# Folding two halves of a PSUM sum with a copy and an add, and turning it with transposes, in a graph attention network

## The chip, the cores and the metric

The kernel runs on one core of one Trainium2 chip. The metric is the device time of one launch in microseconds, as the median of several timed runs; less is better. Beside the timed runs there is one profiled run, from which all views of the profile come.

## The reference

Four layers of a graph network follow one another on 3327 nodes with 256 features each. The adjacency matrix has 3327 x 3327 entries, about 0.5% of them ones. Layer 0 is a simple attention that fills in the features; layers 1 to 3 are transformer layers, masked by the adjacency:

```python
qkv = layer_norm(x, g1, be1) @ w_qkv            # q, k, v: 8 heads of 32
scores = einsum('nhd,mhd->hnm', q, k) * SCALE
scores = where(adj != 0, scores, -inf)
attn = softmax(scores, axis=-1)
out = einsum('hnm,mhd->nhd', attn, v).reshape(n, 256)
x = x + out @ w_proj + b_proj
h2 = layer_norm(x, g2, be2)
x = x + gelu(h2 @ w1 + b1) @ w2 + b2            # 256 -> 1024 -> 256
```

Only the neighbours of a node count for its row of `out`. The change touches one place: between `out` and `out @ w_proj`.

## The kernel before

The kernel first reads the adjacency, does layer 0, and makes for each node a list of its neighbours. The nodes are sorted by their number of neighbours and cut into 26 blocks of 128. A block `b` has `CAPS[b]` neighbour slots (40 for the first, 24 to 10 for the others); a slot is one neighbour of each of the 128 nodes. A group is four slots. For each slot an indirect DMA, issued by GpSimd, gathers 128 rows of keys and values from DRAM into a ring of ten group buffers:

```python
def issue(self):
    ...
    t = ring.tile([P, GS * KVW[1]], FP, tag="kv", ...)        # ten buffers
    for s in range(n):                                        # up to 4 slots
        nc.gpsimd.indirect_dma_start(out=t[:, s, :], in_=kv[L], ...)   # L1226
```

VectorE multiplies keys by queries and reduces them to scores; ScalarE takes the exponentials; VectorE multiplies the values by the weights. TensorE then adds the slots up, two at a time: a product of the identity with 512 columns (two slots of 256) is accumulated in a PSUM bank `po`. At the end the bank's left half holds the sum of the even slots, its right half that of the odd ones. The rows of a block are nodes, the columns features:

```python
def values(self, b, s0):
    ...
    if s0 == 0:
        while len(self.po) > 1:            # two banks: a third block waits for the first
            self.short.pop(0)()
        self.po[b] = ps_o.tile([P, 512], FP, tag="o", ...)
    vw = work.tile([P, GS * D], FP, tag="vw", bufs=3, ...)
    nc.vector.tensor_mul(vw, v, wp)                                    # L1289
    for s in range(0, n, 2):
        m = min(2, n - s) * D
        nc.tensor.matmul(self.po[b][:, :m], ident, vw[:, s * D:s * D + m], ...)   # L1294
    self.issue()
    if s0 + GS >= S:
        self.short += self.block(b)
```

When the last group of a block is summed, its short steps are put in a queue: copy the bank to SBUF, bring it into the transposed form that the projection wants as its stationary operand, copy that, project, add to `x`.

```python
def block(self, b):
    ...
    def copy():
        c["o"] = work.tile([P, 2 * D], FP, tag="o", ...)
        nc.scalar.copy(c["o"], self.po[b])                             # L1312

    def turn():
        pt = self.po[b]
        for k in range(2):
            for h in range(2):
                k0 = h * D + k * P
                nc.tensor.matmul(pt[:, k * P:(k + 1) * P], c["o"][:, k0:k0 + P], ident,
                                 start=(h == 0), stop=(h == 1))        # L1319

    def copy_T():
        c["oT"] = work.tile([P, 2 * P], FP, tag="oT", ...)
        nc.scalar.copy(c["oT"], self.po[b][:, :2 * P])                 # L1324

    def project():
        ps = self.po[b][:, D:]
        nc.tensor.matmul(ps, ones_bf[:96, :], bias3[:, 0, :], start=True, stop=False)   # L1328
        for k in range(2):
            nc.tensor.matmul(ps, c["oT"][:, k * P:(k + 1) * P], w["w_proj"][:, k, :],
                             start=False, stop=(k == 1))               # L1330

    def add():
        nc.vector.tensor_add(x, x, self.po.pop(b)[:, D:])              # L1334
        n2.stats(chunk.index(b), x)
        if b == chunk[-1]:
            self.long += self.chunk(chunk, n2)     # the feed-forward part of up to 4 blocks
            ...
    return [copy, turn, copy_T, project, lambda: None, add]
```

The product of `turn` with the identity as the moving operand transposes a 128 x 128 piece; two of them, one from each half, accumulate into one place, so the halves are added while they are turned.

The feed-forward part of a chunk of blocks (norm, `up` into banks `pu` at L1373, `gelu` on ScalarE at L1379, `down` into `py` at L1396, transposes back into `pd` at L1410, the next layer's queries, keys and values at L1426) makes up the long queue. The loop takes a turn per group: scores, values of an earlier group, then steps of both queues. The order of instructions on each engine is as the program writes it.

```python
def some(self):
    if self.short:
        self.short.pop(0)()
    self.credit = min(self.credit + self.rate, 8.0)
    while self.long and self.credit > 0:
        cost, step = self.long.pop(0)
        self.credit -= cost
        step()
    if self.short:
        self.short.pop(0)()

def run(self):
    ...
    for k, b in enumerate(ORDER):          # blocks with few and many slots in turn
        for g in slots[b]:
            self.scores(*g)                                            # L1248, L1249
            if g == slots[b][-1]:
                self.softmax(b)
                ...
            for _ in range(2 if len(todo) > NBUF // 2 or b == 0 else 1):
                if todo and wait[todo[0][0]] > 1:
                    value()
            self.some()
        ...
```

Of the kernel before, what the change touches and what calls it, by code (L numbers as in the profile page):

```python
# [8 lines left out]
FP = mybir.dt.float32  # L9
# [8 lines left out]
P = 128  # L18
N = 3327
D = 256  # L20
# [503 lines left out]
def sparse_path(ctx, tc, ins, out, dram, flag):  # L524
    nc = tc.nc
# [3 lines left out]
    ident = const.tile([P, P], FP, name="s_ident")  # L529
# [93 lines left out]
    with tc.tile_pool(name="a", bufs=1) as a, tc.tile_pool(name="aw", bufs=2) as aw, \  # L623
# [44 lines left out]
        o = 0  # L668
# [364 lines left out]
        for i in range(NB):  # L1033
# [8 lines left out]
            k = 1 if i < NB - 2 else 2  # L1042
# [54 lines left out]
        for i in range(NB):  # L1097
            nc.tensor.matmul(pp[:, :2 * NB], oh_lo[:, i, :],
                             ids[:, i, :, :].rearrange("p a b -> p (a b)"),
                             start=(i == 0), stop=(i == NB - 1))  # L1100
# [35 lines left out]
    work = ctx.enter_context(tc.tile_pool(name="b_work", bufs=2))  # L1136
# [63 lines left out]
    class Layer:  # L1200
# [101 lines left out]
        def block(self, b):  # L1302
            L, w, c = self.L, self.w, {}
            x = t2[:, b, :D]
            chunk = CHUNK[b]
            if b == chunk[0]:
                self.n2 = Norm(len(chunk), f"f{L}_{b}")
            n2 = self.n2

            def copy():  # L1310
                c["o"] = work.tile([P, 2 * D], FP, tag="o", name=f"o_{L}_{b}")
                nc.scalar.copy(c["o"], self.po[b])  # L1312

            def turn():
                pt = self.po[b]
                for k in range(2):
                    for h in range(2):
                        k0 = h * D + k * P
                        nc.tensor.matmul(pt[:, k * P:(k + 1) * P], c["o"][:, k0:k0 + P], ident,  # L1319
                                         start=(h == 0), stop=(h == 1))  # L1320

            def copy_T():
                c["oT"] = work.tile([P, 2 * P], FP, tag="oT", name=f"oT_{L}_{b}")
# [13 lines that stand above are left out]
                    self.long += self.chunk(chunk, n2)  # L1337
                    at = ORDER.index(b) + 1
                    turns = sum(len(slots[i]) for i in ORDER[at:at + CB])
                    turns = 5 if at == NB - 1 else turns - 2  # L1340
                    self.rate = sum(cost for cost, _ in self.long) / max(turns, 1)

            return [copy, turn, copy_T, project, lambda: None, add]

        def chunk(self, blocks, n2):
            L, w, nxt = self.L, self.w, self.nxt
# [221 lines left out]
```

## Time and profile before

| what | value |
|---|---|
| timed, median of 3 | 2904.16 us (2901.46 to 2905.93) |
| profiled execution, span | 3329.9 us |
| mean granted TensorE clock in it | 0.791 |
| stage before the attention layers, in the profile | about 660 us |
| the three attention layers, in the profile | about 2670 us |

The profiled execution is longer than the timed ones. PE is TensorE's matmul row and PEld its weight loads, DVE is VectorE, ACT is ScalarE, POOL is GpSimd. A row of a group names the line, the engine, the operation, what is written from what, and the count, then busy time and mean duration, then the time the engine stood idle just before and what ended it. A row of a wait names who waited for whom, the sum in us, how often, and the longest. "issue" is time in which an engine waited for nothing that the profile shows; "remote" and "another core or an unknown queue" are releasers that the profile can't name.

### The profile page before, as it was taken

What the parts mean: (1) busy time and instruction counts of PE and PEld (TensorE: products, weight loads), DVE (VectorE), ACT (ScalarE), POOL (GpSimd) and SP (SyncE); (2) the same over time, 40 slices, a digit from 0 to 9 for tenths busy, and PEclk for the clock granted to TensorE, in tenths of its full rate; (3) what the DMA queues carried; (4) which work ended last, traced back from release to release, by engine and by line L of the source; (5) the groups of instructions that cost most, each with busy time, mean ns of one, the idle gap of its engine ahead of it and who ended that gap; (6) DMA issues with size and microseconds to landing.
All of it is one profiled execution on the core that took longest, in us unless ns stands there. A gap on an engine that the chain in (4) does not pass through costs nothing.

```text
span 3329.9 us, 22700 instructions
## 1 busy us (share of the span) xinstructions
PE 2138.1 (64%) x6859; PEld 1150.0 (35%) x6859; DVE 1957.7 (59%) x4063; ACT 767.3 (23%) x1335; POOL 1362.9 (41%) x1461
## 2 busy tenths in 40 slices
PE   4566666135678677774356887878733656767566
PEld 4444444013334333342123333333421323323234
DVE  3977774545666746743546667676444656557453
ACT  3344442001222222221012222222310211212111
POOL 3000000364555645511645555456035465556550
PEclk9676667567788889787678898888876887888788
DMA  4233321464556646533645556556145454545450
GB/s 175 103 109 109 121 76 53 139 185 139 156 154 178 186 133 168 167 71 95 176 130 151 150 156 173 148 153 179 31 134 159 133 169 137 161 137 165 140 142 13
DMA packets 144482, 453.73 MB, mean 136 GB/s; under 512 B 29521, under 2 KB 40156, under 8 KB 141021
## 3 DMA queue, kind: packets, MB, share of 16 engines
q0 software_dynamic: 113056, 370.26, 39.7%
q1 hardware_dynamic: 9834, 53.90, 4.6%
q10 hardware_dynamic: 21458, 28.02, 2.3%
q8 instruction: 56, 0.92, 0.1%
q14 instruction: 78, 0.64, 0.1%
HBM read 420.64 MB, written 31.42 MB: 136 GB/s over the span
## 4 chain that ended last, share of the span: by engine, by line
PE 20%; DVE 14%; issue 13%; POOL 9%; another core or an unknown queue 9%; DMA 3%; ACT 2%; DVEq 0%; POOLq 0%; SPq 0%; ACTq 0%
POOL kv L1226 9%; PE po L1294 7%; DVE kv L1248 4%; PE pu L1373 4%; PE py L1396 3%; DVE vw L1289 3%; DVE sc L1249 3%; DMA kv<-kv,t 3%; PE pk L1426 2%; PE po L1330 1%; PE po L1319 1%; PE pq L1426 1%; DVE st_f L575 0%; DVE t L1334 0%
## 5 line engine op out<-in xcount | busy, mean ns | idle before, releaser
L1226 POOL DMA_INDIRECT kv<-kv,t x1344 | 1276.8, 950 | 1243.9 <-issue 532.1
L1294 PE MATMUL po<-vw,s_ident 128*128 128x512 f32 (+1 forms) x1380 | 790.8, 711 | 493.1 <-DVE vw L1289 350.3
L1294 PEld LDWEIGHTS po<-vw,s_ident 128*128 128x128 f32 x1380 | 298.4, 228 | 854.1 <-issue 497.5
L1248 DVE TENSOR_TENSOR kv<-kv,q 128x1024 f32<-128x1024 f32 (+3 forms) x363 | 413.0, 1138 | 137.5 <-DMA kv<-kv,t 50.4
L1334 DVE TENSOR_TENSOR t<-t,po 128x256 f32<-128x256 f32 x78 | 32.8, 420 | 677.3 <-PE po L1330 287.2
L1249 DVE TENSOR_REDUCE sc<-kv 128x32 f32<-128x1024 f32 (+3 forms) x363 | 414.1, 1141 | 13.5 <-DVE kv L1248 1.1
L1289 DVE TENSOR_TENSOR vw<-kv,w 128x1024 f32<-128x1024 f32 x333 | 371.8, 1128 | 76.7 <-remote 59.8
L1373 PE MATMUL pu<-fT,s_w 128*128 128x512 f32 (+3 forms) x768 | 318.2, 548 | 43.3 <-issue 21.3
L1396 PE MATMUL py<-gT,s_w 128*128 128x512 f32 (+2 forms) x672 | 285.6, 553 | 1.3 <-ACT gT L1379 1.3
L1373 PEld LDWEIGHTS pu<-fT,s_w 128*128 128x128 f32 x768 | 152.9, 210 | 194.7 <-issue 151.9
L1379 ACT ACTIVATE gT<-pu,pvb 128x512 f32<-128x512 f32 (+3 forms) x192 | 115.9, 609 | 310.4 <-PE pu L1373 168.7
L702 POOL MEMSET s_abf<- 128x1 bf16 x26 | 2.6, 104 | 434.8 <-PE s_ptb L714 251.3
L1312 ACT COPY o<-po 128x512 f32<-128x512 f32 x78 | 45.7, 586 | 547.9 <-PE po L1294 276.1
L1396 PEld LDWEIGHTS py<-gT,s_w 128*128 128x128 f32 x672 | 128.5, 194 | 125.4 <-issue 106.3
L1319 PE MATMUL po<-s_ident,o 128*128 128x128 f32 x624 | 101.7, 314 | 94.8 <-ACT o L1312 65.0
L714 PE MATMUL s_ptb<-s_ident_bf,s_abf 128*128 128x128 bf16 x676 | 76.5, 291 | 116.0 <-ACT s_aT L715 80.4
L1319 PEld LDWEIGHTS po<-s_ident,o 128*128 128x128 f32 x624 | 92.3, 221 | 137.4 <-ACT o L1312 88.1
L1330 PEld LDWEIGHTS po<-s_w_proj,oT 128*128 128x128 f32 x312 | 62.3, 222 | 184.3 <-issue 176.5
L1426 PE MATMUL pk<-s_w_qkv,nT 128*128 128x512 f32 x208 | 116.7, 690 | 10.6 <-issue 7.0
L1328 PE MATMUL po<-bias,s_ones_bf 96*128 96x256 bf16 x78 | 23.3, 299 | 155.2 <-issue 98.8
L724 DVE MAX8 cand<-s_v 128x8 f32<-128x208 bf16 x416 | 117.6, 361 | 0.9
L1324 ACT COPY oT<-po 128x256 f32<-128x256 f32 x78 | 29.1, 373 | 371.1 <-remote 215.1
(284 smaller groups left out, 2486.2 us busy)
## 6 DMA issues: line engine op xcount, KB each, us to landing
s_a<-in_adj_dram SPq DMA_DIRECT2D x25, 1663.5 KB
kv<-kv,t POOLq DMA_INDIRECT x1344
kv<-kvr ACTq DMA_DIRECT2D x52, 256.0 KB
kv<-s_kvr ACTq DMA_DIRECT2D x26, 256.0 KB
s_w<-in_L_gnn_w_dram SPq DMA_DIRECT2D x6, 1024.0 KB
t<-ql ACTq DMA_DIRECT2D x6, 592.0 KB
t<-s_x ACTq DMA_DIRECT2D x6, 512.0 KB
s_w_qkv<-in_L_gnn_w_qkv_dram SPq DMA_DIRECT2D x3, 768.0 KB
```

What stands on the lines that cost most here:

```text
L724: nc.vector.max(out=self.cand[:, s, :], in_=v[:, s, :])
L1226: nc.gpsimd.indirect_dma_start(out=t[:, s, :], out_offset=None, in_=kv[L], in_offset=bass.IndirectOffsetOnAxis(ap=t2[:, b, k:k + 1].bitcas ...
L1248: nc.vector.tensor_mul(k, k, self.q[b][:, None, :].to_broadcast([P, n, D]))
L1249: nc.vector.tensor_reduce(self.sc[b][:, s0:s0 + n, :], k.rearrange("p s (h d) -> p s h d", d=HD), AX.X, ALU.add)
L1289: nc.vector.tensor_mul(vw[:, :n * D].rearrange("p (s h d) -> p s h d", h=HEADS, d=HD), v, self.wp[b][:, s0:s0 + n, :, None].to_broadcast([ ...
L1294: nc.tensor.matmul(self.po[b][:, :m], ident, vw[:, s * D:s * D + m], start=(s0 + s == 0), stop=(s0 + s + 2 >= S), skip_group_check=True)
L1319: nc.tensor.matmul(pt[:, k * P:(k + 1) * P], c["o"][:, k0:k0 + P], ident, start=(h == 0), stop=(h == 1))
L1330: nc.tensor.matmul(ps, c["oT"][:, k * P:(k + 1) * P], w["w_proj"][:, k, :], start=False, stop=(k == 1))
L1373: nc.tensor.matmul(c["pu", f][:, :n], w["w1"][:, e, f * P:(f + 1) * P], c["hT"][:, e, :n], start=(e == 0), stop=(e == 1))
L1379: nc.scalar.activation(g[:, :n], c.pop(("pu", f))[:, :n], AF.Gelu_apprx_tanh, bias=w["b1"][:, f:f + 1])
L1396: nc.tensor.matmul(c["py"][e][:, :n], w["w2"][:, f, e * P:(e + 1) * P], g[:, :n], start=(f == 0), stop=last)
L1426: nc.tensor.matmul(ps[:, :c1 - c0], c["hT"][:, e, j * P:(j + 1) * P], nxt["w_qkv"][:, e, c0:c1], start=(e == 0), stop=(e == 1))
```

## The change

The halves are added before they are turned. ScalarE copies only the left half of the bank to SBUF, VectorE adds the right half to it in place, and TensorE turns the sum with two transposes in place of four accumulating products. `o` takes half the room in SBUF. It is for less work on TensorE and ScalarE, at the price of one more instruction on VectorE. The queue of short steps gets two empty places ahead of and behind the copy, so that the steps stand further apart.

```diff
             def copy():
-                c["o"] = work.tile([P, 2 * D], FP, tag="o", name=f"o_{L}_{b}")
-                nc.scalar.copy(c["o"], self.po[b])
+                c["o"] = work.tile([P, D], FP, tag="o", name=f"o_{L}_{b}")
+                nc.scalar.copy(c["o"], self.po[b][:, :D])
+
+            def fold():
+                nc.vector.tensor_add(c["o"], c["o"], self.po[b][:, D:])
 
             def turn():
-                pt = self.po[b]
                 for k in range(2):
-                    for h in range(2):
-                        k0 = h * D + k * P
-                        nc.tensor.matmul(pt[:, k * P:(k + 1) * P], c["o"][:, k0:k0 + P], ident,
-                                         start=(h == 0), stop=(h == 1))
+                    nc.tensor.transpose(self.po[b][:, k * P:(k + 1) * P],
+                                        c["o"][:, k * P:(k + 1) * P], ident)
 ...
-            return [copy, turn, copy_T, project, lambda: None, add]
+            return [lambda: None, copy, lambda: None, fold, turn, copy_T, project, lambda: None, add]
```

## The prediction

> **What bounds the kernel now.** I read four views, in this order: busy time by engine, the waits, the chain that ended last (whole, then inside the layers), and the groups of the lines that change. One number comes first. The profiled execution takes 3329.9 us and the timed one 2904.16 us, so some 426 us of what the profile shows is not in the time to be predicted.
>
> Busy time by engine over the whole span:
>
> ```profile
> PE 2138.1 (64%) x6859; PEld 1150.0 (35%) x6859; DVE 1957.7 (59%) x4063; ACT 767.3 (23%) x1335; POOL 1362.9 (41%) x1461
> ```
>
> No engine is full. The first 660 us belong to the stage that reads the adjacency, which the change doesn't touch; the three attention layers share the other 2670 us. By stretch (columns: stretch, length, then busy us and instructions of PE, PEld, DVE, ACT, POOL, then the granted clock, DMA share and GB/s), the middles of the three layers and one layer's start and end look like this:
>
> ```profile
> 900.00:1400.00 500.00, 382.96 (x989) 180.46 (x988) 314.14 (x554) 127.02 (x281) 273.18 (x289) 0.85 0.59 165
> 1560.00:1700.00 140.00, 43.58 (x98) 20.30 (x98) 78.37 (x114) 9.27 (x22) 85.32 (x89) 0.62 0.57 164
> 1700.00:2280.00 580.00, 445.24 (x1177) 217.08 (x1178) 369.39 (x618) 138.44 (x242) 307.12 (x324) 0.87 0.54 156
> 2280.00:2440.00 160.00, 122.85 (x374) 68.99 (x372) 71.65 (x148) 40.55 (x75) 33.17 (x35) 0.85 0.30 73
> 2700.00:3200.00 500.00, 337.90 (x870) 161.52 (x870) 311.09 (x475) 95.16 (x158) 288.20 (x304) 0.83 0.53 154
> ```
>
> In the middles TensorE is busiest (77%, 77%, 68%), VectorE follows with 62 to 64%. GpSimd looks lower (53 to 58%), but each gather has 950 ns busy and an "issue" gap of about 300 ns after it, so a gather takes 1.25 us of GpSimd: the 304 GpSimd instructions of the last of these stretches, nearly all gathers, are 380 of 500 us, 76%. TensorE and GpSimd are about equally near to being a bound. The chain says the same. Over the whole span, by engine:
>
> ```profile
> PE 20%; DVE 14%; issue 13%; POOL 9%; another core or an unknown queue 9%; DMA 3%; ACT 2%; DVEq 0%; POOLq 0%; SPq 0%; ACTq 0%
> ```
>
> Asked for 900 to 1400 us alone, by line, its largest parts are TensorE's value sums (12.5%) and its feed-forward products; for 1700 to 2280 us they are "issue" 29.7% and the gathers 25.1%. So TensorE sets the pace in part of the time, gather issue in another part, and neither alone. The waits that touch the changed lines:
>
> ```profile
> PE po L1294 <- DVE vw L1289: 350.3, 89, 19.9
> DVE t L1334 <- PE po L1330: 287.2, 35, 28.1
> ACT o L1312 <- PE po L1294: 276.1, 48, 28.1
> ACT oT L1324 <- PE po L1319: 93.5, 43, 6.1
> PE po L1319 <- ACT o L1312: 65.0, 27, 9.4
> PE po L1328 <- ACT oT L1324: 56.4, 19, 18.0
> ```
>
> TensorE waits for VectorE's weighted values, and VectorE waits at its add (L1334) for TensorE: the two run in each other's wake. ScalarE stands still at the copy `o` until the sums are done, and TensorE stands still for that copy 27 times, 65 us in all.
>
> [...] each fp32 product leaves two matmul records and each transpose one; four products (x8 records) take 1.05 us at the full clock and four transposes of `pd` (x4) take 0.60 us. [...] the trace has 586 ns for 512 and 373 for 256, a difference of 213. [...]
>
> **The change part by part.** There are 78 blocks (26 in each of three layers).
>
> ```profile
> L1319 PE MATMUL po<-s_ident,o 128*128 128x128 f32 x624 | 101.7, 314 | 94.8 <-ACT o L1312 65.0 <-issue 29.8
> ```
>
> *TensorE, removed.* The row above, from the groups by form: 624 records, that is 78 x 4 products of two records, 101.7 us busy, or 1.30 us a block (the 314 ns of one record overlap). *Added:* 2 transposes a block. The transposes of `pd` are 150 records with 24.4 us busy, 0.163 us each; those of `pf` and `pn` 260 records with 62.5, 0.24 each, but these wait on ScalarE between pairs. I choose 0.18: 156 x 0.18 = 28 us. Net 101.7 - 28 = **-74 us of TensorE**.
>
> *ScalarE.* 78 x (586 - 373) ns = **-17 us**.
>
> *VectorE.* 78 adds of 128x256, one operand in PSUM, 420 ns each by L1334: **+33 us**.
>
> *Order.* A turn of the loop takes one short step, some feed-forward steps, and a second short step. Before, the six steps of a block fill three turns: copy, turn | copy_T, project | nothing, add. After, nine steps fill four and a half: nothing, copy | nothing, fold | turn, copy_T | project, nothing | add. So (a) the copy now comes behind the turn's feed-forward steps, and ScalarE runs its gelus before it stops for the sums; (b) the transposes come a turn after the fold, so TensorE finds their operand ready: the 65 us of waits on the copy should go; (c) VectorE gets a new place to wait, the fold, a turn behind the copy; (d) the add comes one and a half turns later, but its distance from the projection is one turn as before. With two PSUM banks for `po`, the next-but-one block needs the bank when its values begin; the shortest block has three groups, the softmax delay adds about two turns, so by my count of turns the nine steps are never pulled forward.
>
> *What lies on the end-setting path.* TensorE has 20% of 3330 = 666 us on the chain out of 2138 busy, so 31% of its work counts; VectorE 466 of 1958, 24%; ScalarE 67 of 767, 9%. Then: TensorE -74 x 0.31 = -23; VectorE +33 x 0.24 = +8; ScalarE -17 x 0.09 = -1.5; waits on the copy -65 x 0.31 = -20, of which I keep half, -10, since most of them fall at layer starts and ends where something else is waited for next; new waits at the fold, say +6, an estimate without a row behind it. Sum about -20 us: **2884 us**, -0.7%.
>
> **The rivals.** *TensorE is the bound almost everywhere in the timed runs.* For: it is the busiest engine, and 9% of the chain has no owner in the profile; if those 286 us belong to the 426 that the timed runs don't have, the engines stand closer together there. Then all 74 us in the layers count and most of the copy waits: -80 to -110, about 2805 to 2825. Against: 55% of the chain in the second layer's middle is gathers and issue gaps. *Gather issue is the bound.* For: 1344 gathers x 1.25 us = 1680 us, and GpSimd also idles about 125 us at each layer boundary, out of some 2330 timed us in the layers (2904 x 2670/3330). Then TensorE's relief is hidden, and the time stays within 10 us of 2904. Against: GpSimd waits 386.9 us for VectorE to free ring slots. *The fold is a worse wait than the one removed.* [...] if TensorE and ScalarE trail by more than a turn at the fold, the scores behind it wait, ring slots free later, and gathers stop. For: VectorE already waits 287 us at its add, mean 8 us. Against: that lag is shared by both waits; one stop at the fold shortens the next at the add. This would make it 2915 to 2950.
>
> **Range and chances.** The main sum and the gather-bound rival lie between 2880 and 2905, the TensorE rival reaches below 2846 (2% faster), the fold rival rarely above 2962. I put 10% on faster by over 2%, 86% within 2%, 4% slower; and the range 2850 to 2915.
>
> **What would show it.** L1319 with 156 matmul records and about 28 us busy; `o` at 373 ns; a new VectorE row at about 420 ns x78; TensorE's wait at L1319 for `o` nearly gone; VectorE waits split between fold and add with about the same sum. I am wrong if that sum grows by more than 50 us, if GpSimd's wait for VectorE grows, or if TensorE's busy time falls by 74 and the span by as much or more.

## The result, and the profile after

| kernel | timed, median of 3 | ratio to before (95%) |
|---|---|---|
| before | 2904.16 us (2901.46 to 2905.93) | |
| after | 2887.17 us (2885.01 to 2888.34) | 0.994 [0.992, 0.996] |

The change takes 17 us off, 0.6%. The prediction said 2884 us.

The profile of the changed kernel spans 2886.5 us. First the busy time by engine, from its page:

```profile
PE 2003.6 (69%) x6391; PEld 1062.0 (37%) x6391; DVE 1981.0 (69%) x4141; ACT 791.8 (27%) x1363; POOL 1359.1 (47%) x1461
```

TensorE and VectorE are now equally busy. The rows of the changed lines, from the groups by form:

```profile
L1319 PE MATMUL po<-s_ident,o 128*128 128x128 f32 x156 | 33.5, 300 | 18.2 <-DVE o L1315 18.2
L1312 ACT COPY o<-po 128x256 f32<-128x256 f32 x78 | 28.7, 368 | 118.5 <-PE po L1294 118.4
L1315 DVE TENSOR_TENSOR o<-o,po 128x256 f32<-128x256 f32 x78 | 32.4, 415 | 41.6 <-ACT o L1312 41.6
L1334 DVE TENSOR_TENSOR t<-t,po 128x256 f32<-128x256 f32 x78 | 32.5, 417 | 99.7 <-PE po L1330 95.2 <-ACT q L1234 4.4
L1379 ACT ACT_TABLE_LOAD x51 | 65.4, 1283 | 0.9
L1263 ACT ACT_TABLE_LOAD x50 | 64.2, 1283 | 0.9
```

TensorE's line fell from 624 records and 101.7 us to 156 and 33.5 us; the copy is down to 368 ns; the new fold (L1315) costs VectorE 32.4 us. The two rows of table loads were x37 and x36 before: the new order makes ScalarE change between the exponential (L1263) and the gelu (L1379) 28 times more, 36 us that nobody had planned.

The waits of the changed kernel that touch these lines, and those of VectorE at the first instruction of a group of scores (L1248):

```profile
DVE kv L1248 <- DMA kv<-kv,t: 152.9, 73, 7.0
DVE kv L1248 <- ACT q L1234: 144.3, 40, 7.3
ACT o L1312 <- PE po L1294: 118.4, 20, 21.8
POOL kv L1226 <- DVE vw L1289: 98.7, 33, 10.3
DVE t L1334 <- PE po L1330: 95.2, 35, 6.6
DVE o L1315 <- ACT o L1312: 41.6, 14, 12.1
```

VectorE stands still at the fold only 14 times out of 78. What it waits for instead is, first of all, gathered keys and the queries: it has got ahead of the work that feeds it.

One thing must be known before the profiles are compared. The same kernel takes quite different times on different chips: the kernel before took 2904 us on the chip of the timed result and 2906 us on the chip of the last two experiments, but 3340 to 3365 us on the two chips of the ten experiments ahead of them. I call the first kind *quick chips* and the second *slow chips*; that it is the chip, and not something else that came with it, is the likeliest reading and not shown apart. The first profile of before (3329.9 us) has the length that a slow chip gives it, and no profile of before on a quick chip exists. Ratios are to runs of before on the same chip.

The profiles of the slow chips also lack part of the signals by which one engine releases another: in the first profile of before TensorE's program raises its semaphore 1245 times and the record has 1041 of these, for ScalarE 885 of 1209, for VectorE 2556 of 3169. The profiles of the quick chips have all of them. So waits and releasers that were read from a slow chip, the prediction's among them, are less certain than those of the changed kernel here.

### The profile page after: what moved, and what is told of

Read it like the earlier page. It is cut to its first block, busy times and chain, and to the rows that moved or that the text cites. A ratio compares the mean times of both kernels' runs of the same rounds, so it can differ in the third digit from the quotient of the medians.

```text
span 2886.5 us, 21905 instructions
## 1 busy us (share of the span) xinstructions
PE 2003.6 (69%) x6391; PEld 1062.0 (37%) x6391; DVE 1981.0 (69%) x4141; ACT 791.8 (27%) x1363; POOL 1359.1 (47%) x1461
## 3 DMA queue, kind: packets, MB, share of 16 engines
q0 software_dynamic: 113056, 370.26, 45.7%
## 5 line engine op out<-in xcount | busy, mean ns | idle before, releaser
L1294 PE MATMUL po<-vw,s_ident 128*128 128x512 f32 (+1 forms) x1380 | 778.2, 700 | 493.5 <-DVE vw L1289 443.6
L1248 DVE TENSOR_TENSOR kv<-kv,q 128x1024 f32<-128x1024 f32 (+3 forms) x363 | 413.4, 1139 | 309.7 <-DMA kv<-kv,t 152.9
L1294 PEld LDWEIGHTS po<-vw,s_ident 128*128 128x128 f32 x1380 | 286.3, 221 | 845.3 <-issue 476.5
L1373 PE MATMUL pu<-fT,s_w 128*128 128x512 f32 (+3 forms) x768 | 302.4, 527 | 1.0 <-ACT fT L596 1.0
L1379 ACT ACTIVATE gT<-pu,pvb 128x512 f32<-128x512 f32 (+3 forms) x192 | 116.6, 608 | 350.7 <-PE pu L1373 350.2
L714 PEld LDWEIGHTS <-s_abf 128*128 128x128 bf16 x676 | 65.4, 135 | 128.9 <-issue 94.7
L1426 PE MATMUL pk<-s_w_qkv,nT 128*128 128x512 f32 x208 | 106.4, 636 | 8.8 <-ACT nT L596 8.8
L588 ACT ACTIVATE xn_f<-t,nm_f,rqy_f 128x256 f32<-128x256 f32 x78 | 42.9, 593 | 247.6 <-DVE nm_f L582 238.3
L1263 ACT ACTIVATE sc<-sc,mx 128x120 f32<-128x120 f32 (+6 forms) x78 | 31.9, 410 | 260.9 <-DVE mx L1260 257.1
L1334 DVE TENSOR_TENSOR t<-t,po 128x256 f32<-128x256 f32 x78 | 32.5, 417 | 99.7 <-PE po L1330 95.2
L715 ACT COPY s_aT<-s_ptb 128x896 bf16<-128x896 bf16 x104 | 83.3, 853 | 64.6 <-PE s_ptb L714 64.6
L1186 POOL DMA_INDIRECT t<-t,perm x26 | 24.6, 946 | 158.6 <-DMA colsb<-in_L_gnn_be_dram 151.0
L1414 DVE TENSOR_TENSOR t<-t,pd 128x256 f32<-128x256 f32 x75 | 29.5, 408 | 93.3 <-PE pd L1410 93.3
```

Source lines behind the costliest of these rows:

```text
L714: nc.tensor.transpose(pt[:, m, :], self.abf[:, k * P:(k + 1) * P], ident_bf)
L715: nc.scalar.copy(aT[:, k0:k0 + len(ks), :], pt[:, :len(ks), :])
L1248: nc.vector.tensor_mul(k, k, self.q[b][:, None, :].to_broadcast([P, n, D]))
L1373: nc.tensor.matmul(c["pu", f][:, :n], w["w1"][:, e, f * P:(f + 1) * P], c["hT"][:, e, :n], start=(e == 0), stop=(e == 1))
L1379: nc.scalar.activation(g[:, :n], c.pop(("pu", f))[:, :n], AF.Gelu_apprx_tanh, bias=w["b1"][:, f:f + 1])
L1426: nc.tensor.matmul(ps[:, :c1 - c0], c["hT"][:, e, j * P:(j + 1) * P], nxt["w_qkv"][:, e, c0:c1], start=(e == 0), stop=(e == 1))
```

## The experiments

**The theories.** The change has two parts, an arithmetic (copy a half, fold, transpose) and an order (nine places in the queue where there were six). *Theory A*, the prediction's: the gain is TensorE's relief, and the order is neutral or helps a little. *Theory B*: the two parts work against each other; one gains much, the other gives most of it back. *Theory C*: the gain is the copy moved away from its wait for the sums, and the arithmetic gives nothing.

### Does the kernel before repeat, and what is each part worth alone?

The kernel before, profiled once more:

> The kernel before once more, unchanged, for a second profile: the first had a span of 3329.9 us where the timed runs take 2904, the profile of the changed kernel has 2886.5 and its timed runs 2887. If the 426 us are stalls of that one execution, this profile has a span near 2905 us and no 'remote' waits worth naming. If profiling the old kernel always costs this much, it is near 3330 us again.

This one execution took 3366 us, with a span of 3364.2 us, and eleven others of the same kernel on the same chip took 3362 us in the median. So the long time is not a stall of one execution. Nor is it the profile: the profiled execution of the changed kernel was one of its timed ones (2888.34 us).

The order alone, with the old arithmetic (an edit of before):

```diff
-            return [copy, turn, copy_T, project, lambda: None, add]
+            return [lambda: None, copy, lambda: None, lambda: None, turn, copy_T, project,
+                    lambda: None, add]
```

> The old copy of the whole bank and the old four adding products, but in nine places as in the changed kernel, with an empty one where the fold stands. The program then switches between the exp and gelu tables 51 times as the changed kernel does, 37 before. Theory A (the gain is TensorE's smaller work, the order is neutral): 2899 to 2909 us. Theory B (the later order costs time by the 28 extra table loads of 1.28 us each, and hides a larger gain of the arithmetic): 2912 to 2930. Theory C (the gain is the copy moved away from the wait for the sums, the arithmetic gives nothing): 2882 to 2892.

Measured on a slow chip: 3481.89 us, ratio 1.034 [1.031, 1.038].

The arithmetic alone, in the old six places (an edit of after; fold and transposes share one place):

```diff
-            return [lambda: None, copy, lambda: None, fold, turn, copy_T, project, lambda: None, add]
+            return [copy, lambda: (fold(), turn()), copy_T, project, lambda: None, add]
```

> The new arithmetic (half copy, fold, two transposes) in the old six places: copy in the first, fold and transposes together in the second. 37 table switches as before. Theory A: 2882 to 2892 us. Theory B: 2860 to 2878. Theory C: 2900 or more, since TensorE then waits in the same turn for a copy and a fold.

Measured on the same chip: 3270.87 us, ratio 0.972 [0.969, 0.976]. And with eight places, the first empty one left out:

```diff
-            return [lambda: None, copy, lambda: None, fold, turn, copy_T, project, lambda: None, add]
+            return [copy, lambda: None, fold, turn, copy_T, project, lambda: None, add]
```

> The changed kernel with eight places in place of nine: copy, nothing, fold, transposes, copy_T, project, nothing, add. 41 table switches where the changed kernel has 51; the fold still comes a turn after the copy, the transposes some feed-forward steps after the fold. Theory A: 2882 to 2892 us. Theory B: 2865 to 2880. Theory C: 2890 to 2900, since the copy stands ahead of the gelus again.

Measured: 3311.27 us, ratio 0.985 [0.981, 0.989]. On this chip theory B holds in direction: the arithmetic gains 2.8%, the order loses 3.4%, and the product of both, 1.034 x 0.972 = 1.006, should be the whole change. In size it had expected less of either (0.3 to 0.9% of loss, 0.9 to 1.5% of gain). Theories A and C, by which the order is neutral or gains, fall here.

### The whole change on a slow chip, and the table loads

The changed kernel, and the arithmetic alone, on the second slow chip:

> The changed kernel, unchanged, beside the kernel before on one chip. In the last call the kernel before took 3362 us on its chip where it had taken 2904, so only ratios on one chip are compared. Order alone gave 1.0345 there and arithmetic alone 0.9723. If the two parts add up (theory B), a chip as slow as that one gives a ratio of about 1.0345 x 0.9723 = 1.006; a chip that runs the kernel before in about 2904 us gives 0.994 again. Theory A expects 0.994 on any chip.

> The new arithmetic in the old six places, a second time, to stand beside the changed kernel on one chip. Theory B: 0.965 to 0.98 and clearly below the changed kernel. Theory A: equal to the changed kernel within 0.5%.

The whole change took 3368.46 us, ratio 1.008 [1.005, 1.011]: slower here, where it was 0.994 on the quick chip. The arithmetic alone took 3257.77 us, ratio 0.974 [0.971, 0.978]. So the sign of the whole change depends on the chip.

First suspect for the cost of the order (B1): the 28 further table changes. In the next two kernels the gelu is left out and a tanh takes its place, so the output is another. Of table loads at L1263 and L1379 (46.2 and 47.5 us in before) their profiles show no row among the groups of 15.3 us busy and more. The first is an edit of after, the second of before:

```diff
-AF.Gelu_apprx_tanh
+AF.Tanh
```

> The changed kernel with tanh in place of gelu: same size and count of ScalarE instructions, but [...] the program has no table switch in the layers. It leaves the gelu out, so its output isn't the reference's. To be read against the next run: theory B1 (the table loads are what the new order costs) expects a ratio of this to the next of 0.965 to 0.98, as arithmetic alone had; theory B2 (the order costs by the gelus that wait for TensorE ahead of exp and the query copy in ScalarE's queue) expects 0.99 to 1.01, as the change had with gelu.

> The kernel before with tanh in place of gelu, likewise without table switches and without the gelu's result. Its 73 table loads of 1.28 us are 94 us of ScalarE; if they matter by themselves (B1), 0.96 to 0.985 of the kernel before; if not (B2), 0.99 to 1.0.

Ratios to the (unedited) kernel before: 1.006 [1.004, 1.007] and 1.000 [0.998, 1.002]. Without those loads the new kernel still stands 0.5% behind the old one. B1 falls; the loads cost nothing that shows in the time. That they lie where ScalarE waited anyway was not shown.

### The queries, and seven places

Second suspect (B2): VectorE's wait at L1248 for `q`, a copy that stands on ScalarE behind the gelus (284 us of waits with the order alone, the first line, 60 us in before, the second, both on a slow chip):

```profile
DVE kv L1248 <- ACT q L1234: 284.2, 17, 29.5
DVE kv L1248 <- ACT q L1234: 59.6, 26, 10.2
```

The copy goes to VectorE (an edit of after):

```diff
-            nc.scalar.copy(self.q[b], t2[:, b, D:2 * D])
+            nc.vector.tensor_copy(self.q[b], t2[:, b, D:2 * D])
```

> The changed kernel with the copy of the next block's queries (78 times 128x256) taken from ScalarE and given to VectorE, at the same place of the program. Tanh in place of gelu moved the time by 0.5% and less, so table loads aren't what the new order costs. Theory B2 (in the new order the query copy stands behind gelus that wait for TensorE, and VectorE waits for it: 120 us in 17 waits on the last chip, 60 in the kernel before, 18 with the arithmetic alone): 40 to 90 us below the changed kernel on the same kind of chip, so a ratio to the kernel before of 0.98 to 0.995 where the kernel before takes 3350, and below 0.99 where it takes 2904. Theory B3 (the order costs because each chunk's feed-forward part starts one and a half turns later, so that six to eight of its steps fall behind the last gather of a layer and VectorE's waits only move): no gain, and up to 25 us more for VectorE's 78 copies.

Ratio 1.007 [1.004, 1.009] on a slow chip, the same as the whole change (1.008, on the other slow chip). B2 falls there. It was not tried on a quick chip, where the changed kernel waits 144.3 us for `q`.

Seven places, both empty ones left out (an edit of after):

```diff
-            return [lambda: None, copy, lambda: None, fold, turn, copy_T, project, lambda: None, add]
+            return [copy, fold, turn, copy_T, project, lambda: None, add]
```

> The new arithmetic in seven places: copy, fold, transposes, copy_T, project, nothing, add. TensorE no longer has to wait for the fold in the same half turn (118 us with the arithmetic alone in six places), and the add comes half a turn later than before in place of one and a half. Theory B: as good as the arithmetic alone or better, a ratio of 0.965 to 0.98 where the kernel before takes about 3350 us, 0.975 to 0.99 where it takes 2904. Theory A: 0.994 or the ratio of the changed kernel.

3267.46 us, ratio 0.971 [0.968, 0.973], no worse than six. On slow chips the time grows with the places: 0.971 at seven, 0.985 at eight, 1.008 at nine.

### The last two, on a quick chip

Two suspects were left: that the feed-forward part of a chunk is queued later (B3), or that the short steps themselves come later (B4). The next kernel has the old six places, but queues the feed-forward part five empty places after the add, where the nine places bring it (an edit of after; `push` holds the lines of `add` that extend the long queue):

```diff
-            return [lambda: None, copy, lambda: None, fold, turn, copy_T, project, lambda: None, add]
+            late = [lambda: None] * 5 + [push] if b == chunk[-1] else []
+            return [copy, lambda: (fold(), turn()), copy_T, project, lambda: None, add] + late
```

> The new arithmetic in the old six places, with one thing of the new order brought in alone: each chunk's feed-forward part enters its queue five places later, as late after the chunk's last value as in the changed kernel. By the count of turns the short steps of a block stay as early as in the kernel before (about 2 turns after its last value, 4 turns before the block after the next needs the bank), while 100, 100 and 90 long steps are left after the values of the last gather of each layer (94, 94 and 82 before), and the table is switched 51 times on each of two lines (37 and 36 before). If the late feed-forward is what the order costs, the ratio to the kernel before is 0.995 to 1.01, near that of the whole change, and clearly above the run of the new arithmetic alone beside it. If it is the late short steps, and the bank that comes free within one turn of its next use, the ratio is 0.965 to 0.98, equal to the new arithmetic alone.

> The new arithmetic in the old six places once more, as the measure for the run beside it. On a chip like that of the earlier runs the ratio is 0.97 to 0.977. If this chip takes the kernel before in about 2900 us, the theory that the arithmetic gains and the order gives it back expects a ratio under 0.99 there too; the theory that the order is neutral expects 0.994, the ratio of the whole change.

These two fell on a chip that takes before in 2906.23 us, and both expectations missed. The arithmetic alone took 2953.61 us, ratio **1.017 [1.015, 1.018]**: not a gain of 2.7% but a loss of 1.7%. With the late feed-forward it was 2942.24 us, ratio 1.014 [1.012, 1.016], slightly better, if at all (the intervals touch), and not worse. So on the kind of chip on which the result was measured **both theory A and theory B fall as I had put them**: the arithmetic alone costs 47 us (2953.6 - 2906.2), and the order, brought in on top of it, takes off 64 (from +47 to -17; as a ratio, 0.994/1.017 = 0.978). That last step compares two chips of the same kind, each by its own runs of before. Theory C comes nearest: it had put the arithmetic alone at 2900 us or more. What it expected of the order alone, 2882 to 2892, was not run on such a chip.

**Why, by the profile.** Here are the waits of the arithmetic alone on the quick chip, the counterpart of the waits of the changed kernel above:

```profile
ACT o L1312 <- PE po L1294: 412.3, 78, 21.2
DVE o L1315 <- ACT o L1312: 296.2, 78, 7.7
POOL kv L1226 <- DVE vw L1289: 164.2, 65, 9.6
DVE t L1334 <- PE po L1330: 121.1, 48, 6.0
DVE kv L1248 <- DMA kv<-kv,t: 52.7, 24, 7.0
DVE kv L1248 <- ACT q L1234: 38.9, 23, 3.1
PE po L1319 <- DVE o L1315: 24.8, 27, 0.9
```

The copy waits for the sums every time, 78 of 78, and the fold waits for the copy every time. The fold stands on VectorE, in the program ahead of the next scores, and VectorE stands idle ahead of it for 296.2 us (3.8 us a block), in which the scores behind it don't start (for missing keys they wait only 52.7 us). GpSimd in turn waits 164.2 us for VectorE to free ring buffers. With one empty place ahead of the copy and one ahead of the fold, the 296.2 us become 41.6, and the copy's 412.3 us (78 times) become 118.4 (20 times).

But 255 us less at the fold made the span only 62 us shorter (2948.5 to 2886.5). VectorE's idle time before its lines shows where the rest went; the rows of L1248 and L1315 are on the pages. First the arithmetic alone, then the changed kernel:

```profile
L1248 DVE TENSOR_TENSOR kv<-kv,q 128x1024 f32<-128x1024 f32 (+3 forms) x363 | 412.9, 1138 | 98.7 <-DMA kv<-kv,t 52.7
L1315 DVE TENSOR_TENSOR o<-o,po 128x256 f32<-128x256 f32 x78 | 32.9, 421 | 296.2 <-ACT o L1312 296.2
```

```profile
L1248 DVE TENSOR_TENSOR kv<-kv,q 128x1024 f32<-128x1024 f32 (+3 forms) x363 | 413.4, 1139 | 309.7 <-DMA kv<-kv,t 152.9
```

| idle time of VectorE ahead of | arithmetic alone | changed kernel | difference |
|---|---|---|---|
| the fold, L1315 | 296.2 us | 41.6 us | -254.6 |
| the add, L1334 | 123.3 us | 99.7 us | -23.6 |
| the scores, L1248 | 98.7 us | 309.7 us | +211.0 |
| sum | 518.2 us | 451.0 us | -67.2 |

VectorE's busy time is the same in both (1984.3 and 1981.0 us), so the span less the busy time, all that VectorE idles, fell by 59 us: these three lines by 67, the others rose by 8. Of the 278 us that leave the fold and the add, 211 come back at the scores, about half of it as waits for gathered keys (52.7 to 152.9 us), the next limit, and half as waits for the copy of the queries on ScalarE (38.9 to 144.3 us). The second half is a wait that the order itself brings.

The stretches show the same by time. Cut at the first and last gather of the second layer, the end of that layer, and the end of the program (columns: stretch, length, busy us and instructions of PE, PEld, DVE, ACT, POOL, then clock, DMA share, GB/s); the arithmetic alone:

```profile
1441.00:2132.00 691.00, 500.69 (x1233) 232.44 (x1234) 488.24 (x799) 155.12 (x283) 424.78 (x448) 0.84 0.61 176
2132.00:2247.00 115.00, 81.58 (x271) 49.66 (x269) 46.64 (x126) 32.45 (x63) 0.16 (x1) 0.84 0.17 47
2868.00:2949.00 81.00, 49.23 (x183) 32.56 (x181) 27.53 (x63) 16.30 (x32) 7.37 (x8) 0.84 0.13 29
```

and the changed kernel:

```profile
1410.00:2059.00 649.00, 483.67 (x1220) 228.70 (x1221) 490.78 (x802) 167.12 (x290) 424.15 (x448) 0.85 0.66 187
2059.00:2181.00 122.00, 87.38 (x284) 51.82 (x283) 41.47 (x121) 34.19 (x66) 0.07 (x2) 0.86 0.17 45
2790.00:2887.00 97.00, 64.27 (x209) 38.89 (x207) 28.26 (x66) 18.27 (x36) 7.05 (x8) 0.82 0.10 25
```

The same 448 gathers and the same VectorE work (488 and 491 us) take 691 us in the one and 649 in the other. At 1.25 us from one gather's start to the next (0.95 us busy and 0.30 us of gap, in the timelines of both kernels), the gathers alone are an estimated 560 us of these. The end of the layer is 7 us longer with the late order, the end of the program 16. Over all three layers the gathers' stretches are 691 + 691 + 621 = 2003 and 652 + 649 + 609 = 1910 us: -93, and the ends +8 +7 +16 = +31, together -62. So the late order does cost something at the ends of the layers, some 30 us, and earns three times that in the middles.

The kernel with the late feed-forward alone lies between. Its fold waits less often (its lines are shifted by three from L1379 on):

```profile
ACT o L1312 <- PE po L1294: 415.9, 73, 21.7
DVE o L1315 <- ACT o L1312: 234.6, 55, 12.7
```

Its stretches sum to -35 us in the middles and its ends to +25 against the arithmetic alone, -10 in sum, about what the timed runs give (-11). So the late feed-forward is not a net cost (B3 falls on this chip), and most of the order's gain is not the feed-forward's: the rest of it comes with the places of the short steps.

### What the slow chips measured

Why do the same edits have the other sign there? The slow chips add long stretches in which TensorE, VectorE and ScalarE all show nothing. One, from the timeline of before on a slow chip (start, length, engine, line, and in brackets the idle time before it and its releaser; POOL lines are gathers):

```profile
732.63 0.59 PE L1330 MATMUL po<-s_w_proj,oT 128*128 128x256 f32 x2
...
734.61 1.99 PE L1294 MATMUL po<-vw,s_ident 128*128 128x512 f32 x4 [1.39 <-issue]
...
736.03 0.20 ACT L1252 CAST t<-kv 128x4 int32<-128x4 f32 x1 [4.91 <-DMA kv<-kv,t]
736.94 0.96 POOL L1226 DMA_INDIRECT kv<-kv,t  x1 [0.30 <-issue]
...
752.48 0.42 DVE L1334 TENSOR_TENSOR t<-t,po 128x256 f32<-128x256 f32 x1 [17.93 <-remote]
```

The add waits 17.93 us for a projection whose last row in the profile ended near 733.2 us; TensorE's last row of any kind ends at 736.6. The releaser has no name. For 15.9 us nothing but gathers runs. I counted all such stretches of 1 us and more in the layers, one profile for each kernel (the counts shift by up to 13 us with where the layers are taken to begin and whether an engine's waiting instructions count as activity):

| kernel (chip; 1 and 2 are the two slow ones) | span, us | silent stretches, us | span less these |
|---|---|---|---|
| before (slow 1) | 3364.2 | 332 | 3032 |
| before with tanh (slow 2) | 3342.0 | 323 | 3019 |
| arithmetic alone, six places (slow 1, slow 2) | 3275.0, 3245.9 | 228, 202 | 3047, 3044 |
| arithmetic, seven places (slow 1) | 3267.9 | 248 | 3020 |
| arithmetic, eight places (slow 1) | 3307.2 | 315 | 2992 |
| the whole change (slow 2) | 3375.7 | 380 | 2996 |
| order alone (slow 1) | 3490.6 | 365 | 3126 |
| arithmetic alone (quick) | 2948.5 | 43 | 2906 |
| arithmetic, late feed-forward (quick) | 2936.7 | 48 | 2889 |
| the whole change (quick) | 2886.5 | 57 | 2830 |

On the first slow chip the arithmetic alone wins 89 us of span against before, and has 104 us less of silence. On the second, beside before with the tanh (whose time was that of before, 1.000), the arithmetic alone wins 96 us and has 121 less of silence; the whole change loses 34 and has 57 more. Without the silence the order of the three is that of the quick chip: the arithmetic alone last (+15 and +25 us), then before, then the whole change (-23). So for these three the ratios of the slow chips speak of how often a kernel runs into these stops, and say little of what the change does on a quick chip. The order alone is another matter: even without the silence it stands 94 us behind before (3126 against 3032). Nothing here says that the nine places are good for the old arithmetic; the 64 us are what they give on top of the new one. This is a reading of single profiles by subtraction, not an experiment; what causes the stops stays open.

## Why the prediction was right, and where only its sum was

The time was right (2884 predicted, 2887.17 measured), and the sizes of the pieces mostly too. The way in which it got from the pieces to the time was not: it has two terms of -10 us, for the arithmetic and for the order, and measured one after the other they are +47 and -64. That their sum comes near the forecast is luck.

- **TensorE, -74 us busy.** Measured -68.2 (101.7 - 33.5). A transpose took 33.5/156 = 0.215 us, not 0.18; a product took 101.7/312 = 0.326 us. That is a factor of 1.5 between them.
- **ScalarE, -17 us.** The copy's row fell by 17.0 us (45.7 - 28.7), as predicted. The 28 table loads more (+36 us) were overlooked; with the tanh in place of the gelu they turned out to cost nothing that shows, on a slow chip (B1). On the quick chip the kernel with the late feed-forward has the same 28 loads more and is not slower than the one without (2942.24 us against 2953.61).
- **VectorE, +33 us.** Measured 32.4.
- **The weights of the path: -23 for TensorE, +8 for VectorE, -1.5 for ScalarE, with +6 for the fold's waits: -10 for the arithmetic.** This is the step that failed: it adds the arithmetic and the order as if either were worth the same without the other. The arithmetic alone, in the old places of a quick chip, came out at +47 us. Whatever TensorE's relief is worth, the same edit put a new stop on VectorE, 296.2 us of waits at the fold, on all 78 blocks; the prediction had sized this stop for the finished change alone. What the arithmetic is worth in the new places stays unmeasured, since the old arithmetic in nine places was not run on a quick chip. The shares of the chain were read from a profile of a slow chip besides, in which 9% had no owner.
- **The order, -10 us, from half of TensorE's waits on the copy.** The mechanism under (a), that the copy then comes behind the turn's gelus and ScalarE no longer stops for the sums, and under (b), that TensorE finds its operand ready, were right in direction: the copy's waits fell from 412.3 to 118.4 us between the arithmetic alone and the change, and TensorE waits 18.2 us at L1319. But of (b) the order brings little, for with the arithmetic alone these waits were 24.8 us already. The size was off: on top of the new arithmetic the order is worth 64 us, six times the -10, and by the idle times chiefly because it gives VectorE, not TensorE, an operand that is there.
- **(c), a new place to wait a turn behind the copy, "+6".** 41.6 us of waits, times the prediction's own 24% for VectorE, is 10: near enough for the whole change. The rival *the fold is a worse wait than the one removed* is what the arithmetic alone does: 2915 to 2950 was its range, 2953.6 the measurement. In the change as made, the two empty places keep it away on a quick chip; on a slow one VectorE still waits 236.6 us at the fold.
- **(d), the add one and a half turns later.** Wrong in size. Counting the turns of the emission, the mean distance from a block's last value to its add grows from 2.0 turns to 4.9, since 26 blocks of nine places fill nearly all of the 242 places that 121 turns offer, and a queue that is nearly full runs late. The copy moves likewise, by 1.3 turns and not only behind the feed-forward steps of its own turn. On the quick chips the ends of the layers are some 30 us longer for it.
- **The rivals.** TensorE was not the bound (2805 to 2825). Gather issue is the bound in part: of what VectorE no longer loses at the fold and the add it loses 211 us at L1248, 100 of them on gathers.
- **What would show it wrong.** "VectorE waits split between fold and add with about the same sum" can't be tested: after has 41.6 + 99.7 = 141 us, but before has no profile on a quick chip. The same holds for GpSimd's wait for VectorE, 98.7 us now. The third sign, a span that falls by as much as TensorE's busy time, did not come: 17 us against 68.

**What stays open.** What the order alone does to the old arithmetic on a quick chip was not run, nor seven and eight places there, nor the queries' copy on VectorE. Why the arithmetic alone loses 47 us and not more or less can't be taken apart further without a quick profile of before. One more term may be in it: the mean granted TensorE clock in the runs of the last chip was 0.828 to 0.833 for before and 0.818 to 0.822 for both new kernels, 1.2% lower. If all of TensorE's 2030 us counted, that would be some 24 us, an estimate from these numbers; it was not separated. It doesn't part the arithmetic alone from the whole change, whose clock was 0.816 to 0.821.

## What to carry to other kernels

When work moves to an engine at the head of the pipeline, look first at whether its operand is there when its turn comes: here 33 us of new VectorE work brought 296 us of waiting at the old distance and 42 us with one empty place ahead of the copy and one ahead of the fold. An edit of the arithmetic and the spacing that goes with it should be measured together and apart, because a part by itself can have the other sign, and two parts need not add up. And a part's worth must be measured on the kind of chip on which the result was: ten runs on slow chips gave a consistent story that two runs on a quick one turned round, while the one part not run there, the order alone, leaves the account open.

## What the runs showed of the hardware that I had not expected

The same kernel took 2904 to 2906 us on some chips and 3340 to 3365 us on others. The stage ahead of the layers is untouched by this: in its first 635 us the changed kernel on a quick chip, the first line, has the same work as before on a slow one, the second:

```profile
0.00:635.00 635.00, 372.93 (x2142) 268.19 (x2142) 421.76 (x1512) 228.16 (x277) 36.75 (x69) 0.72 0.29 102
```

```profile
0.00:635.00 635.00, 371.96 (x2142) 267.77 (x2142) 421.91 (x1512) 228.18 (x277) 36.80 (x68) 0.72 0.29 102
```

The loss lies in the layers, much of it in the silent stretches (332 us against 43 to 57), at similar places in each of the three layers: in before the longest ones begin at 736.6, 1674.4 and 2581.5 us, each some 100 us after its layer's first gather, and last 15.9, 17.1 and 17.1 us. The granted clock differs by much less than the time (0.79 against 0.82 to 0.83, and 15%). Single instructions of VectorE and single gathers take the same time on both: 1138 ns at L1248 and 950 ns a gather in before, 1139 and 947 ns in the changed kernel. The wait shown above ends some 19 us after the last row of the product that it is for. But about a fifth of the signals of TensorE, ScalarE and VectorE is missing from the records of the slow chips, so it stays open where the time goes, and whether the stops and the missing signals have one cause.
